# Second router in lots of two chunks, and transfers moved ahead at the seams of two expert stages

## The chip, the cores and the metric

One core of a Trainium2 chip. The metric is the device time of one execution in microseconds (us), as the median of several runs. The kernel is one launch: a stack of layers on 64 sequences of 64 positions with 256 features (4096 tokens), all in fp32.

## The reference

Cut to what matters here, with `x` of shape (64, 64, 256):

```python
x = x + attention(conditioned_scan(x, cond))
x = x + ffn0(modulated_linear(x, cond))
x = x + mamba(rnn(x))
x = x + swiglu_experts(shared_and_routed_experts(x, cond))
```

The last line is the subject. Its inner part is a mixture of experts (`_L1_cond2_ref`): a router takes the two best of eight experts for each token from sigmoid scores of the token and of `cond`; the routed experts compute `gelu(x W1) W2` with 256 hidden features; two shared experts, which all tokens pass, compute `(silu(x s1) * (x s3)) s2` with 512 hidden features each; the sum of both parts is divided by 4. Its outer part (`_L1_ffn_ref`) takes that result as its tokens: scores `xt @ Wg.T`, again the two best of eight, experts `(silu(x W1) * (x W2)) W3` with 704 hidden features, their outputs weighted with the scores themselves. The final line adds the residual.

## The kernel before

**Stages.** The program runs the layers one after the other. Tokens are handled in `NCH` = 8 chunks of `CH` = 512; a chunk holds `TT` = 4 groups of 128 tokens (one token to a partition), and `NTT` = 32 groups are all tokens. The residual lies in DRAM (`g.x`, which the profile calls x_mid), features on partitions.

**Mamba with the shared experts beside it.** `mamba` walks over the eight chunks, 32 steps (`STEPS`) each. A step is an exponential on ACT (L871), a product on POOL (`hb`, L864), two scans on DVE (L903), a product on DVE (L905), and transposes that gather the result on PE (L919), with one broadcast matmul `cb` (L818) for the step after. `finish` and `project` (L826 to L844) end a chunk: they make the layer's output, add it to the residual, and store that to x_mid. In a chunk's loop the pieces of a generator, `Mixture.beside` of the chunk before, are taken at the end of each step: `BESIDE` = 56 pieces spread over the 32 steps (L941). What is left of the generator runs at the end of the chunk (L943), behind `urgent`, which holds `project`. These pieces are: scores of the first router (L1389), after half of the chunks the choice of experts (`choose`, L1401), the sending of rows of an earlier chunk to the experts' regions (`send`, L1429, whose rows are scattered at L1100), and the matmuls of the shared experts (L1459 for s1 and s3, L1475 for s2), whose rows are stored to a DRAM buffer, shared_rows (L1481).

**The rest of the first router.** After mamba, `Mixture.rest` (L1484) reads the last chunk back (`xlast`), scores it, chooses for the second half of the tokens, sends the chunks 4 to 7, and runs the last chunk's shared experts between.

**Routing.** `Routing.choose` works on n groups of 128 tokens at once: about 27 small DVE operations, two matmuls (L1067, L1068) and a cast on POOL (L1076) give each token and each of its two experts a row in a DRAM buffer with a region for each expert (moe_x for the first, ffn_x for the second). `Routing.send` scatters a chunk with eight indirect DMAs on POOL's queue (L1100). `Routing.tiles` (L1123) turns the counts into a table of at most `NTL` = 39 tiles of 256 rows: expert and first row of each.

**Expert tiles.** `Experts.run` (L1204) goes over the 39 tiles. `load(i)` reads the tile's two table entries into registers of SP's queue, and issues the loads of the expert's weights and of the tile's rows `gx` (L1107) there; the load of rows waits for all scatters of that router. `turn` transposes the rows (L1224), `up` and `down` are the two matrix products, and `give` scatters the results to a DRAM buffer by token (L1112, on POOL). Load(i+2) is issued between `up(i)` and `down(i)`. `Gelu` is the first router's, with weights `r`; `Swiglu` the second's, with weights `w`.

**Combination and second router.** For each chunk, `Mixture.combine` reads the chunk's shared rows (L1503) into a tile x2 and the two routed rows of each token (`fetch`, L1120, 1 MB a chunk, into one of three buffers `rows2`), and adds them on DVE (L1507). `Gate.chunk` (L1520) transposes the sum, scores it (L1182 to L1192), chooses (n = 4 groups), and scatters the chunk. The tiles x2 have three buffers and are what the scatters read. After all chunks come `tiles` and the Swiglu tiles. The final loop (L1559) reads for each chunk the two expert rows of each token (rows3, three buffers) and the residual (x3, three buffers), transposes and sums on PE (L1569), adds on DVE (L1578) and stores.

**What sets the order.** A scheduler that goes by program order as priority and by due times puts the instructions of each engine into one fixed order[...]. Direct loads and stores all go through SP's queue, in order, and a load that waits holds what is behind it. Pools give tiles their memory: a pool opened in memory that another pool has just given up waits for that pool's last readers.

Of the kernel before, what the change touches and what calls it, by code (L numbers as in the profile page):

```python
# [19 lines left out]
P = 128  # L20
# [663 lines left out]
def mamba(g, w, hs, beside):  # L684
# [11 lines left out]
    LEFT = 40  # L696
    BESIDE = 56
    nc.scalar.activation(w.A, w.A, AF.Exp)
    nc.vector.tensor_scalar(w.A, w.A, -1.0, None, ALU.mult)
    hs2 = hs.rearrange("p k b t -> p k (b t)")  # L700
    seq = lambda t: t.rearrange("p (b l) -> p b l", l=L)
    with (
# [186 lines left out]
        for s in range(LAST):  # L889
# [45 lines left out]
            while left < (j + 1) * LEFT // (STEPS - AHEAD):  # L935
# [4 lines left out]
                mid = got  # L940
            for _ in range((j + 1) * BESIDE // STEPS - j * BESIDE // STEPS):  # L941
                next(others, None)
# [6 lines left out]
NE = 8  # L949
# [59 lines left out]
class Routing:  # L1009

    def __init__(self, g, pool, x, name, most):

        nc = g.nc
        self.g, self.x, self.name, self.most = g, x, name, most
        self.sent, self.made = [], []
# [20 lines left out]

        self.goes_on = pool.tile([P, NE, most], F32, name="goes_on")
        nc.gpsimd.memset(self.goes_on, 1.0)  # L1040
        nc.gpsimd.memset(self.goes_on[:, :, 0:1], 0.0)

        self.row = pool.tile([P, 2, NTT], mybir.dt.int32, name="row")

    def choose(self, t0, sel, tags, work):


        nc = self.g.nc
        n = self.most
        wide = lambda t: t.unsqueeze(1).to_broadcast([P, n, NE])  # L1050
# [9 lines left out]
        nc.vector.tensor_tensor(mine, by(masks[0]), by(masks[1]), ALU.add)  # L1060
        nc.vector.tensor_tensor_scan(flat(upto), flat(self.goes_on), flat(mine), 0.0, ALU.mult, ALU.add)
        nc.vector.tensor_sub(mine, upto, mine)
# [133 lines left out]
class Experts:  # L1196
# [6 lines left out]

    def run(self, tables):  # L1204
        g, nc = self.g, self.g.nc
        S = TR // P
        table, rank = tables

        def load(i):
            v = SimpleNamespace()  # L1210
            SP = mybir.EngineType.SP
            e = in_order(g.tc, table[0:1, 0, i : i + 1], [SP], NE - 1)
            row = in_order(g.tc, table[0:1, 1, i : i + 1], [SP], NE * REG)
            self.weights(v, e)
            v.x = self.pw.tile([P, S, RW], F32, name="gx")
            self.routing.read(v.x, row)
            v.i, v.rank = i, rank[:, i : i + 1]
            return v

# [30 lines left out]

        now = load(0)
        turn(now)
        after = load(1)
        for i in range(NTL):
            self.up(now)
            if i + 1 < NTL:
                turn(after)
            nxt = load(i + 2) if i + 2 < NTL else None
            down(now)
            now, after = after, nxt  # L1260
# [94 lines left out]
class Mixture:  # L1355

    HALF = NCH // 2

    def __init__(self, g, pool, x):
        nc, a = g.nc, g.a
        self.g = g
        self.routing = Routing(g, pool, x, "moe", NTT // 2)
        self.Wr = pool.tile([P, 2 * KD, NE], F32, name="Wr")
# [18 lines left out]
    def beside(self, c, x, work):  # L1384

        g = self.g
        pt = scores(g, work, self.Wr[:, :KD, :], x, self.cond[:, ts(c, CB)])  # L1389
        g.nc.scalar.copy(self.score[:, ts(c, TT), :], pt)  # L1390
        yield
        if (c + 1) % self.HALF == 0:
            self.choose(c // self.HALF, work)
            yield
        if c >= self.HALF:
            yield from self.send(c - self.HALF, work)
            if c == NCH - 2:
                yield from self.send(c - self.HALF + 1, work)
        yield from self.shared(c, x, work)

    def choose(self, half, work):  # L1401
        nc = self.g.nc
        n = NTT // 2
        t0 = half * n
        s = work.tile([P, n, NE], F32, name="score")
# [78 lines left out]
    def rest(self, work):  # L1484

        g = self.g
        x = work.tile([P, KD, CH], F32, name="xlast")
        g.nc.sync.dma_start(x, g.x[:, :, (NCH - 1) * CH :])
        pt = scores(g, work, self.Wr[:, :KD, :], x, self.cond[:, (NCH - 1) * CB :])
        g.nc.scalar.copy(self.score[:, (NCH - 1) * TT :, :], pt)  # L1490
        self.choose(1, work)
        others = self.shared(NCH - 1, x, work)
        for c in range(self.HALF, NCH):
            for _ in self.send(c, work):
                for _ in range(4):
                    next(others, None)
        for _ in others:
            pass

    def combine(self, c, rows, work):  # L1500

        nc = self.g.nc
        nc.sync.dma_start(rows, self.made[ts(c, CH), :].rearrange("(t p) d -> p t d", p=P))  # L1503
        got = work.tile([P, TT, 2, D], F32, name="rows2")
        self.routing.fetch(c, got)
        for j in range(2):
            nc.vector.tensor_add(rows, rows, got[:, :, j, :])  # L1507


class Gate:  # L1510


    def __init__(self, g, pool, x):
# [3 lines left out]
        nc.sync.dma_start(self.Wg, g.a["ffn1_WgT"].rearrange("(k p) n -> p k n", p=P))  # L1517
        self.routing = Routing(g, pool, x, "ffn1", TT)

    def chunk(self, c, rows, work):  # L1520
# [7 lines left out]
        pt = scores(g, work, self.Wg, x)  # L1528
        s = work.tile([P, TT, NE], F32, name="score")
        sel = work.tile([P, TT, NE], F32, name="gsel")  # L1530
        nc.vector.tensor_copy(s, pt)
        nc.vector.tensor_copy(sel, s)
        masks = self.routing.choose(c * TT, sel, rows[:, :, D:], work)
        for j in range(2):
            mine = work.tile([P, TT, NE], F32, name="mine")
            nc.vector.tensor_mul(mine, s, masks[j])
            nc.vector.tensor_reduce(rows[:, :, WT + j], mine, AX.X, ALU.add)
        self.routing.send(c, rows)


def mixtures(g, mix, x, out):

    nc, tc = g.nc, g.tc
    with ExitStack() as ctx:
        pool = lambda name, bufs: ctx.enter_context(tc.tile_pool(name=name, bufs=bufs))
        p1 = pool("e1", 1)
        gate = Gate(g, p1, x)
        with ExitStack() as first:
            pool1 = lambda name, bufs: first.enter_context(tc.tile_pool(name=name, bufs=bufs))
            q1, q2, q3, qw = pool1("q1", 1), pool1("q2", 2), pool1("q3", 3), pool1("qw", 3)  # L1550
            mix.rest(q2)
            Gelu(g, mix.routing, (q2, q3, qw)).run(mix.routing.tiles(q1))
            for c in range(NCH):
                rows = q3.tile([P, TT, RW], F32, name="x2")
                mix.combine(c, rows[:, :, :D], q3)
                gate.chunk(c, rows, q2)
        p2, p3, pw = pool("g2", 2), pool("g3", 3), pool("gw", 3)
        Swiglu(g, gate.routing, (p2, p3, pw)).run(gate.routing.tiles(p1))
        for c in range(NCH):  # L1559
            rows = p3.tile([P, TT, 2, D], F32, name="rows3")  # L1560
            gate.routing.fetch(c, rows)
            x = p3.tile([P, KD, CH], F32, name="x3")
            nc.sync.dma_start(x, g.x[:, :, ts(c, CH)])
            for k in range(KD):
# [25 lines left out]
def tile_adaln_attn_ffn_d2(ctx: ExitStack, tc: tile.TileContext, a: dict, out: bass.AP):  # L1590
# [18 lines left out]
    ffn0(g, w_ffn0)  # L1609

    p_hs, close_hs = scoped(tc, "hs", side="right")
    hs = p_hs.tile([P, KD, B, L], F32, name="hs")
    rnn(g, w_rnn, hs)
    close_mid()
    close_x()
    p_mix, close_mix = scoped(tc, "w_mix")
    mix = Mixture(g, p_mix, rows[0])
    close_banks()
    with tc.tile_pool(name="beside", bufs=1) as work:
        mamba(g, w_mamba, hs, lambda c, x: mix.beside(c, x, work))  # L1620
    close_hs()
    close_banks = banks(g)

    mixtures(g, mix, rows[1], out)
    close_banks()
    close_mix()
    close_mamba()

# [77 lines left out]
```

## Time and profile before

| | us |
|---|---|
| median of 3 runs | 3241.16 (3240.91 to 3246.52) |
| the profiled execution | 3242.95, of it 3241.2 in the profiled span |
| mamba, last scan (L903) | ends 2117.6 |
| first scatter and last scatter of `rest` | 2173.5, 2225.2 |
| Gelu tiles: first matmul, last scatter | 2242.8, 2424.9 |
| second router: first scatter, end of last scatter | 2447.2, 2545.6 |
| Swiglu tiles: first transpose, last scatter | 2557.3, 3183.2 |
| end of the span | 3241.2 |

Times in the lower rows are counted from the start of the span. They come from the timeline and the rows of single lines. In a group's row, "x64 | 64.3, 1005 | 20.5 <-issue 17.1" says: 64 instructions, 64.3 us busy, 1005 ns each, 20.5 us in which the engine stood idle just before them, most of it not put down to another engine. In a row of waits, "28.0, 6, 9.0" are the total, the number and the longest. The engines are PE (matmul), PEld (its weight load), DVE, ACT, POOL and SP (which issues DMAs).

### The profile page before, as it was taken

Reading aid. Unit: us, or ns where it says so; the run is one execution under the profiler, and the core shown is the slowest. Engines: PE = TensorE matmul, PEld = TensorE weight load, DVE = VectorE, ACT = ScalarE, POOL = GpSimd, SP = SyncE. Lnnn points to the kernel's source line nnn. Section 1 sums busy time; section 2 is a strip of 40 time slices with the busy share of each in tenths; the row PEclk is TensorE's granted clock in tenths of the full one; section 3 lists DMA queues with packets and bytes.
Section 4 is the critical chain, followed back from the end, with each engine's and each line's share of the span. In section 5 each row is a group of like instructions: output and inputs, shape, how many; then the busy total and the mean of one; then the engine's idle time right before and its main releaser. Section 6 shows DMA issues by size and latency. Waiting matters only on the chain. (4 is left out here: it accounts for less than half of the span.)

```text
span 3241.2 us, 38871 instructions
## 1 busy us (share of the span) xinstructions
PE 2586.4 (80%) x13918; PEld 1807.0 (56%) x13932; DVE 1757.8 (54%) x2860; ACT 1421.5 (44%) x2380; POOL 1308.3 (40%) x1091
## 2 busy tenths in 40 slices
PE   1978886777957788888778888677984599999995
PEld 1534443445734455555455555555761388888885
DVE  0166556884049988898978797731335322222221
ACT  0444443775456575766566666522331112222220
POOL 0011213542046766767577777824445311111110
PEclk9889997878967899999889899898996799999997
DMA  9598000000111212121122122224765655555545
GB/s 220 185 374 331 2 2 0 17 20 30 40 40 64 80 63 75 56 81 69 56 69 82 62 89 73 85 71 134 234 201 186 205 172 168 170 175 169 167 137 195
DMA packets 246305, 376.59 MB, mean 116 GB/s; under 512 B 45712, under 2 KB 147152, under 8 KB 245856
## 3 DMA queue, kind: packets, MB, share of 16 engines
q1 hardware_dynamic: 232480, 336.60, 32.1%
q0 software_dynamic: 13632, 37.50, 3.1%
q8 instruction: 110, 1.80, 0.2%
q14 instruction: 83, 0.68, 0.1%
HBM read 250.81 MB, written 123.22 MB: 115 GB/s over the span
## 5 line engine op out<-in xcount | busy, mean ns | idle before, releaser
L864 POOL TENSOR_TENSOR hb<-dx,Bn 128x1024 f32<-128x1024 f32 x256 | 601.1, 2358 | 267.2 <-PE yp L919 257.1
L903 DVE TENSOR_TENSOR_SCAN hb<-dA,hb 128x512 f32<-128x512 f32 x512 | 603.5, 1210 | 50.1 <-ACT dA L871 47.5
L871 ACT ACTIVATE dA<-delta,A 128x504 f32<-128x504 f32 x512 | 344.1, 683 | 293.4 <-DVE hb L903 290.7
L919 PEld LDWEIGHTS yp<-ident,hb 128*128 128x128 f32 x2048 | 270.1, 153 | 167.5 <-issue 128.1
L1335 PE MATMUL ps<-gxT,w 128*128 128x256 f32 x1560 | 360.3, 387 | 0.8 <-DVE gxT L1226 0.8
L905 DVE TENSOR_TENSOR hb<-hb,cb 128x1024 f32<-128x1024 f32 x256 | 312.3, 1220 | 78.6 <-PE cb L818 60.9
L1335 PEld LDWEIGHTS ps<-gxT,w 128*128 128x128 f32 x1560 | 292.7, 191 | 63.0 <-issue 25.2
L1459 PE MATMUL mq<-x,moe_s 128*128 128x256 f32 x896 | 258.5, 423 | 59.0 <-ACT up L1466 44.3
L919 PE MATMUL yp<-ident,hb 128*128 128x128 f32 x2048 | 304.4, 293 | 1.0 <-ACT yT L931 1.0
L1112 POOL DMA_INDIRECT ffn_y<-gy,to x78 | 74.8, 959 | 563.8 <-ACT gy L1248 559.4
L1339 DVE TENSOR_TENSOR gh<-gs,ps 128x256 f32<-128x256 f32 x195 | 81.2, 417 | 322.0 <-ACT gs L1338 321.1
L1459 PEld LDWEIGHTS mq<-x,moe_s 128*128 128x128 f32 x896 | 176.1, 212 | 121.1 <-ACT up L1466 51.4
L1247 PE MATMUL acc<-w,gh 128*128 128x256 f32 x936 | 230.1, 388 | 0.6 <-ACT gy L1248 0.6
L354 POOL TENSOR_TENSOR E<-E,z 128x1024 f32<-128x1024 f32 x32 | 60.8, 1900 | 417.3 <-DMA moe_x<-fill 204.8
L1248 ACT ACTIVATE gy<-acc,wt 128x256 f32<-128x256 f32 x156 | 73.9, 473 | 341.9 <-PE acc L1247 341.9
L1247 PEld LDWEIGHTS acc<-w,gh 128*128 128x128 f32 x936 | 168.4, 189 | 44.7 <-issue 25.5
L818 PE MATMUL cb<-parts,pick 80*128 80x512 bf16 x256 | 106.7, 417 | 94.7 <-DVE hb L905 79.5
L1338 ACT ACTIVATE gs<-ps 128x256 f32<-128x256 f32 x195 | 74.7, 383 | 231.7 <-PE ps L1335 226.3
L1236 DVE TENSOR_TENSOR to<-at,pick 128x2 int32<-128x2 f32 x78 | 12.6, 161 | 219.5 <-DMA ffn_y<-gy,to 125.5
L1112 POOL DMA_INDIRECT moe_y<-gy,to x78 | 74.8, 959 | 123.4 <-ACT gy L1248 121.0
L372 PE MATMUL acc<-oT,Wout 128*128 128x512 f32 x256 | 114.9, 608 | 9.3 <-ACT oT L366 9.3
L1475 PE MATMUL mq<-moe_s,sh 128*128 128x256 f32 x448 | 116.3, 398 | 4.8 <-ACT up L1466 4.8
(387 smaller groups left out, 4661.6 us busy)
## 6 DMA issues: line engine op xcount, KB each, us to landing
w<-in_ffn_W_dram SPq DMA_DIRECT2D x117, 640.0 KB, 4.6
Bn<-B SPq DMA_DIRECT2D x128, 512.0 KB, 3.6
moe_x<-fill SPq DMA_DIRECT2D x129, 260.0 KB, 5.0
ffn_x<-fill SPq DMA_DIRECT2D x129, 260.0 KB, 6.2
r<-in_moe_r_dram SPq DMA_DIRECT2D x78, 256.0 KB, 3.3
gx<-moe_x SPq DMA_DIRECT2D x39, 260.0 KB, 3.5
gx<-ffn_x SPq DMA_DIRECT2D x39, 260.0 KB, 4.1
x<-x_mid SPq DMA_DIRECT2D x16, 512.0 KB, 5.0
```

Source lines behind the costliest of these rows:

```text
L372: nc.tensor.matmul(ps, wa.Wout[:, o, ts(k, P)], v.o[:, o], start=(o == 0), stop=(o == H // 2 - 1))
L818: nc.tensor.matmul(t, pick[:, n : n + 1].to_broadcast([rows, P]), v.parts, start=True, stop=True)
L864: nc.gpsimd.tensor_mul(hb, vs[c].dx[p], Bn[:, n % NB, :].unsqueeze(1).to_broadcast([P, PI, CH]))
L871: nc.scalar.activation(decays[s][i][:, :, 1:], seq(vs[c].delta[p][:, i, :])[:, :, 1:], AF.Exp, scale=w.A[:, p * PI + i, n : n + 1],)
L903: ins = nc.vector.tensor_tensor_scan(h, dA[i].rearrange("p b l -> p (b l)"), h, 0.0, ALU.mult, ALU.add)
L905: ins = nc.vector.tensor_tensor(hb, hb, cb.unsqueeze(1).to_broadcast([P, PI, CH]), ALU.mult)
L919: nc.tensor.matmul(yp[i][:, t, :], hb[:, i, ts(t, P)], g.ident, start=(n == 0 and t == 0), stop=(n == S - 1 and t == CH // P - 1), is_tran ...
L1112: i = self.g.nc.gpsimd.indirect_dma_start(out=self.y, out_offset=bass.IndirectOffsetOnAxis(ap=to, axis=0), in_=y, in_offset=None)
L1247: nc.tensor.matmul(po[:, s, :], h, w, start=(i == 0), stop=(i == len(parts) - 1))
L1335: nc.tensor.matmul(ps[:, j, :], v.w12[:, k, ts(j * full + i, P)], v.xT[:, k, :], start=(k == 0), stop=(k == KD - 1))
L1459: nc.tensor.matmul(ps[:, i % 2, :], w[:, k, ts(i, P)], xu[:, k, :], start=(k == 0), stop=(k == KD - 1))
L1475: nc.tensor.matmul(ps[:, t, :], h[:, i, ts(t, P)], self.s2[:, i, :], start=(i == 0), stop=(i == NS - 1))
```

## The change

Six edits, all in the two mixtures and what stands next to them.

- In mamba's last chunk 72 pieces are taken beside the steps where the other chunks take 56.
- The first router keeps its lots and sends; they are written as tables (`LOTS`, `SENDS`).
- The second router chooses for two chunks at once (`LOT` = 2, n = 8 groups): `chunk` only scores, and every second chunk `lot` chooses, writes the tags into both chunks' rows with ACT, and sends both. Two copies and a cast of scores go from DVE to ACT.
- The shared rows of all chunks have a tile each (`x2_0` to `x2_7`), read by one function, which `Experts.run` of the Gelu tiles calls after it has issued the loads of tiles 0 and 1 (its new argument `then`). The residual chunks likewise have a tile each (`x3_0` to `x3_7`), read after the loads of Swiglu tiles 0 and 1.
- `load` is split: the weights of tiles 0 and 1 are issued first, and then the rows of tile 0 and of tile 1 (`load_rows`). The pool of the Swiglu weights, `gw`, is opened before the Gelu tiles, so that it takes over no memory of theirs; the tables of the second router are made inside the first part's scope.
- The mixture's weights (`w_mix`) are given memory on the side from which `hs` is taken, before the recurrent layer, and mamba's weights are given up before `mixtures`.

```diff
@@ mamba
+    BESIDE_LAST = 72
...
-            for _ in range((j + 1) * BESIDE // STEPS - j * BESIDE // STEPS):
+            most = BESIDE if c + 1 < NCH else BESIDE_LAST
+            for _ in range((j + 1) * most // STEPS - j * most // STEPS):
                 next(others, None)
@@ Routing
-        n = self.most
+        n = sel.shape[1]
@@ Experts
-    def run(self, tables):
+    def run(self, tables, then=lambda: None):
...
         def load(i):
-            v = SimpleNamespace()
-            SP = mybir.EngineType.SP
-            e = in_order(g.tc, table[0:1, 0, i : i + 1], [SP], NE - 1)
-            row = in_order(g.tc, table[0:1, 1, i : i + 1], [SP], NE * REG)
-            self.weights(v, e)
+            v = SimpleNamespace(i=i, rank=rank[:, i : i + 1])
+            self.weights(v, in_order(g.tc, table[0:1, 0, i : i + 1], [SP], NE - 1))
+            return v
+
+        def load_rows(v):
+            row = in_order(g.tc, table[0:1, 1, v.i : v.i + 1], [SP], NE * REG)
             v.x = self.pw.tile([P, S, RW], F32, name="gx")
             self.routing.read(v.x, row)
...
-        now = load(0)
+        now, after = load(0), load(1)
+        load_rows(now)
         turn(now)
-        after = load(1)
+        load_rows(after)
+        then()
@@ Mixture
+    def shared_rows(self, c, rows):
+        self.g.nc.sync.dma_start(rows, self.made[ts(c, CH), :].rearrange("(t p) d -> p t d", p=P))
+
     def combine(self, c, rows, work):
...
-        nc.sync.dma_start(rows, self.made[ts(c, CH), :].rearrange("(t p) d -> p t d", p=P))
@@ Gate.chunk
-        s = work.tile([P, TT, NE], F32, name="score")
-        sel = work.tile([P, TT, NE], F32, name="gsel")
-        nc.vector.tensor_copy(s, pt)
-        nc.vector.tensor_copy(sel, s)
-        masks = self.routing.choose(c * TT, sel, rows[:, :, D:], work)
+        nc.scalar.copy(self.score[:, ts(c, TT), :], pt)
+        self.rows[c] = rows
+        if (c + 1) % self.LOT == 0:
+            self.lot(c // self.LOT, work)
+
+    def lot(self, i, work):
+        nc = self.g.nc
+        n = self.LOT * TT
+        s = self.score[:, ts(i, n), :]
+        sel = work.tile([P, n, NE], F32, name="gsel")
+        nc.scalar.copy(sel, s)
+        tags = work.tile([P, n, RW - D], F32, name="gtags")
+        masks = self.routing.choose(i * n, sel, tags, work)
         for j in range(2):
-            mine = work.tile([P, TT, NE], F32, name="mine")
+            mine = work.tile([P, n, NE], F32, name="mine")
             nc.vector.tensor_mul(mine, s, masks[j])
-            nc.vector.tensor_reduce(rows[:, :, WT + j], mine, AX.X, ALU.add)
-        self.routing.send(c, rows)
+            nc.vector.tensor_reduce(tags[:, :, WT - D + j], mine, AX.X, ALU.add)
+        for c in range(i * self.LOT, (i + 1) * self.LOT):
+            rows = self.rows.pop(c)
+            nc.scalar.copy(rows[:, :, D:], tags[:, ts(c % self.LOT, TT), :])
+            self.routing.send(c, rows)
@@ mixtures
         gate = Gate(g, p1, x)
+        pw = pool("gw", 3)
...
-            q1, q2, q3, qw = pool1("q1", 1), pool1("q2", 2), pool1("q3", 3), pool1("qw", 3)
-            mix.rest(q2)
-            Gelu(g, mix.routing, (q2, q3, qw)).run(mix.routing.tiles(q1))
+            q1, qw = pool1("q1", 1), pool1("qw", 3)
+            with tc.tile_pool(name="rest", bufs=2) as work:
+                mix.rest(work)
+            q2, q3, qr = pool1("q2", 2), pool1("q3", 3), pool1("qr", 1)
+            rows = [qr.tile([P, TT, RW], F32, name=f"x2_{c}") for c in range(NCH)]
+
+            def shared_rows():
+                for c in range(NCH):
+                    mix.shared_rows(c, rows[c][:, :, :D])
+
+            Gelu(g, mix.routing, (q2, q3, qw)).run(mix.routing.tiles(q1), shared_rows)
             for c in range(NCH):
-                rows = q3.tile([P, TT, RW], F32, name="x2")
-                mix.combine(c, rows[:, :, :D], q3)
-                gate.chunk(c, rows, q2)
-        p2, p3, pw = pool("g2", 2), pool("g3", 3), pool("gw", 3)
-        Swiglu(g, gate.routing, (p2, p3, pw)).run(gate.routing.tiles(p1))
+                mix.combine(c, rows[c][:, :, :D], q3)
+                gate.chunk(c, rows[c], q2)
+            tables = gate.routing.tiles(p1)
+        p2, p3 = pool("g2", 2), pool("g3", 3)
+        px = pool("gx", 1)
+        xs = []
+
+        def residual_chunks():
+            for c in range(NCH):
+                x = px.tile([P, KD, CH], F32, name=f"x3_{c}")
+                nc.sync.dma_start(x, g.x[:, :, ts(c, CH)])
+                xs.append(x)
+
+        Swiglu(g, gate.routing, (p2, p3, pw)).run(tables, residual_chunks)
         for c in range(NCH):
...
-            x = p3.tile([P, KD, CH], F32, name="x3")
-            nc.sync.dma_start(x, g.x[:, :, ts(c, CH)])
+            x = xs[c]
```

## The prediction

> **What bounds the kernel now.** I read the busy times by stage first, since the share over the whole span mixes limits. Columns: window, then PE, PEld, DVE, ACT and POOL busy, the granted PE clock, the DMA share, GB/s.
>
> ```profile
> 2133.00:2166.00 33.00, 15.90 (x60) 10.03 (x59) 5.07 (x17) 4.13 (x7) 5.42 (x28) 0.84 0.36 120
> 2166.00:2243.00 77.00, 54.17 (x232) 44.36 (x232) 11.91 (x47) 20.91 (x30) 42.81 (x48) 0.85 0.29 97
> 2243.00:2424.00 181.00, 165.13 (x776) 133.01 (x776) 62.70 (x305) 60.22 (x117) 74.57 (x79) 0.99 0.72 218
> ...
> 2447.00:2546.00 99.00, 36.83 (x119) 14.66 (x119) 49.60 (x227) 11.63 (x20) 66.31 (x76) 0.62 0.45 150
> 2546.00:2557.20 11.20, 0.00 (x0) 0.00 (x0) 0.12 (x1) 0.00 (x0) 0.00 (x0) 0.50 0.84 263
> 2557.20:3184.00 626.80, 623.80 (x2808) 509.28 (x2808) 151.60 (x546) 127.54 (x313) 74.60 (x78) 0.99 0.50 164
> 3184.00:3241.20 57.20, 26.20 (x128) 24.10 (x128) 10.65 (x16) 0.00 (x0) 0.20 (x1) 0.58 0.79 268
> ```
>
> The tiles (2243 to 2424 and 2557 to 3184) are bound by PE. The change works on the seams between them. At 2546 to 2557 nothing computes; after 3184 the DMA is busiest.
>
> In the second router (2424 to 2560) the groups of instructions put POOL first:
>
> ```profile
> L1100 POOL DMA_INDIRECT ffn_x<-x,row x64 | 64.3, 1005 | 20.5 <-issue 17.1 <-POOL row L1076 3.4
> L1076 POOL CAST row<-rowf 128x8 int32<-128x8 f32 x8 | 1.5, 189 | 20.7 <-DVE rowf L1075 20.6
> L1052 POOL COPY x<-number 128x4 f32<-128x4 f32 x5 | 0.9, 190 | 12.1 <-DMA ffn_x<-x,row 12.1
> ```
>
> 64 scatters at a pace of 1.266 us (0.96 and 0.30 to the next, from the timeline) are 81.0 us. The first starts at 2447.21 and the last ends at 2545.63: 98.4 us, so 17.4 us are gaps, mostly row buffers that come free late (12.1 us on L1052).
>
> The waits before the Swiglu tiles, then those of the final combination:
>
> ```profile
> PE ps L1224 <- DMA gx<-ffn_x: 23.3, 1, 23.3
> ```
>
> ```profile
> PE acc L1569 <- DMA rows<-ffn_y: 28.0, 6, 9.0
> DVE x L1578 <- DMA x<-x_mid: 25.9, 4, 8.3
> ```
>
> Both stand at transfers. And the end of mamba, groups of instructions from the last scan (2117.6) to 2156:
>
> ```profile
> L1459 PE MATMUL mq<-x,moe_s 128*128 128x256 f32 x40 | 10.0, 385 | 1.5 <-ACT up L1466 1.5
> ...
> L1475 PE MATMUL mq<-moe_s,sh 128*128 128x256 f32 x32 | 7.2, 383 | 0.7 <-ACT up L1466 0.7
> ...
> L1182 PE MATMUL ps<-xlast,Wr 128*8 128x512 f32 x2 | 1.9, 1036 | 7.6 <-DMA xlast<-x_mid 7.6
> ```
>
> 72 matmuls of shared experts stand between the last scan and the last chunk's router.
>
> [...] the last scatter ends at 2545.63 and the first weight load that waits for it is issued at 2547.56, 1.93 us later. [...] the trace has 0.19 us for the 128x32 rows. [...]
>
> **Part 1, the last mamba chunk (L941).** 72 pieces go beside the 32 steps instead of 56. In the compiled order 40 matmuls of shared experts are left after the last scan's cb instead of 72: 32 x 0.385 = 12.3 us of PE time move under the scans. Two thirds of these lay on the path: project's last add is at 2132.93, leftover runs to 2147, SP must pass the store of the leftover rows (2147.83) and Wg's load (2150.08) before xlast at 2150.51, and PE has it at 2154.75. After it, the leftover is interleaved with project, which ends near 2137 (8 pairs x 2 x 0.385 is 6 us, part of it in PE's waits); the store and its receipt give xlast's issue at 2140.5, and with the 4.2 us it takes now PE goes on at 2144.7: -10. Cost: 16 more pieces in the chunk. Cover: it has 110.6 us of PE in 148.6 us, the chunk before it 123.7 in 148.0 without being longer; 110.6 + 12.3 stays below that. Without cover all 12.3 come back. The scatters of sends (2) and (3) now come as 8 and 8 in POOL's order where they came 4, then two hb products, then 12: 8 x 1.266 = 10 us in which POOL makes no hb; DVE waited about 11 us at this place before. 0 to +6; I take +1. Sum -9, bounds -13 and 0.
>
> **Part 2, the start of the Gelu tiles.** On SP the reads of shared rows x_0 and x_1 stand ahead of the first table entries, and wait for the first router's scatters, whose memory they take over: so first weights are not ahead of those scatters. The total for the table (2228.63) lies behind PE's shared matmuls as before. The reads go out at about 2228, under the table's DVE work to 2235. Second weights stand before gx0 (two r of 0.26 MB: 1.6 us at 341 GB/s), and six shared reads (3.1 MB, 9.2 us) before tile 2's inputs, with tile 2 due after 2 x 4.47 us: about 1 us of stall. The 341 GB/s are a mean over fully loaded slices just after 2546. Sum +2.5, bounds 0 and +8.
>
> **Part 3, the second router.** Removed: eight reads of shared rows from this stage (4.2 MB) and their wait for row buffers; four of eight chains of about 27 small DVE operations (each lot's are 64 wide, 0.22 against 0.19 us: 4 x 27 x 0.22 = 24 us instead of 8 x 27 x 0.19 = 41, at one place hidden under scatters anyway). The 17.4 us of gaps should shrink to three lot changes of about 0.6 us. But the first scatter waits for two chunks, and in DVE's compiled order the adds of chunks 4 to 7 lie inside lot 0's chain: chunk 7's first add stands before rowf. With three rows2 buffers its fetch goes out only after chunk 4's adds. Now: c0's fetch is in by 2433.2, c3's goes out at 2435.7 and, at 8 us, lands near 2443.7; c4's near 2447, c7's goes out near 2449.5 and lands near 2457.5. Its add (1.2), the rest of the chain and the cast: first scatter at 2462, 15 us later than now. Then 81.0 + 1.8 from 2462.4: end at 2545.2 against 2545.63: -0.4. Bounds -6 (fetches at 6 us) and +6.
>
> **Part 4, the start of the Swiglu tiles.** The tables already ended at 2540.3, before the last scatter; only the loads gain. w(0) and w(1) (2.16 MB each) go out before the last scatters, having buffers of their own. After the last one: 1.9 receipt, 2.6 for a gx alone, PE at +4.6 instead of 2557.30 - 2545.63 = 11.67: -7.0; bounds -8 and -5. Queued behind gx0 and gx1 on SP: eight residual reads (4.2 MB) and then w(2): 4.2 + 2.2 + 0.3 = 6.7 MB, 19.6 us at 341 GB/s. Tile 2 is due 2 x 15.9 us after the start: hidden, by 12 us; uncovered it would cost up to 8, if scatters halve the rate.
>
> **Part 5, the final combination.** Five of eight x reads fell into this stage: 2.6 of its 15.35 MB. The rest at its own 268 GB/s takes 47.5 us (-9.7); at 341 GB/s with 2.6 to start and 2 for the last store, 41.6 (-15.6). What is late next is rows<-ffn_y, held by three buffers and behind the out stores on SP. Walking the SP order gives a last add 11 us earlier: I take -11.3, bounds -15 and -7.
>
> The first weights of the mixture and the moved rcond matmuls: nothing; they landed before B<-dbc (922) in any case. If not covered, at most one load's landing, 5 us.
>
> **Sum.** -9 + 2.5 - 0.4 - 7.0 - 11.3 = -25.2 us, against the profiled execution's 3242.95 us (span 3241.2 and 1.75 around it): 3217.75. The median of the runs is 1.79 lower, so 3216.0. Bounds added in quadrature give about 10 us either way: 3206 to 3226 for this case.
>
> **Rivals.**
> A. The adds of later chunks don't hold lot 0, and only the gaps go. For it: POOL has 17.4 us of gaps. Against it: the order on DVE is fixed. First scatter at about 2447, end near 2530: 15 us more, 3201.
> B. The gain is eaten at three places: hb waits for POOL's scatters (+5), the tile 2 stall at Gelu (+3.5), rows<-ffn_y takes over the waits of x<-x_mid (+4). For it: PE waits 28.0 us for rows<-ffn_y already. Against it: the sum of bytes falls. 3216 + 12.5 = 3228.5.
> C. Slower: lot 0 behind chunk 7's fetch, at the head of the second router. POOL then has no gaps to give, so each us by which the first scatter is later is a us of the whole. It decides from 2494 on (2462 + 32 for 3248). That needs 16 us for each of the two fetches in series instead of 8, or a third fetch in series. For it: the fetches wait for one another's buffers. Against it: 8.0 us was measured with shared reads beside them. About 3250.
> D. It doesn't do what it says: w(0) and w(1) stay behind the scatters of the second router, as the first router's do. Then -7 is lost and the other terms stay: 3223, inside the range.
>
> **How the numbers follow.** The main case, D within it, 0.60; A 0.12; B 0.16, of which 0.04 ends within 0.2%; sundry cancelling to no change 0.05; C 0.07. A measurement of this kernel tells about 0.2% (6.5 us) from no change. Faster 0.84, same 0.09, slower 0.07. The range goes from A's middle (3200) to past B (3236).
>
> **What would show it.** PE's first matmul on xlast 9 us earlier counted from the last scan; first scatter L1100 15 us later counted from the last Gelu scatter and then no wait on L1052; 4 to 5 us from the last L1100 to PE L1224 with w landed before; no DVE wait for x<-x_mid and a stage after the last ffn_y scatter of 46 us. I am wrong if lot 0's chain runs before chunk 7's add, if a step of the last chunk grows, or if tile 2 of either expert stage stalls.

## The result, and the profile after

| | us |
|---|---|
| before, median of 6 runs of the first comparison | 3242.45 (3240.91 to 3247.97) |
| changed, median of 6 runs | 3221.53 (3211.95 to 3226.11) |
| ratio | 0.993, 95% interval 0.9914 to 0.9946 |
| profiled execution of the changed kernel | 3220.07, span 3218.3 |

The change is 20.9 us faster where 25.2 were forecast. How large the gain is depends on more than the code, as the control below shows: in a later group of runs the same kernel was only 8.7 us faster than the kernel before, measured on the same chip as it.

The busy times by stage of the changed kernel, with the columns of before (window, length, PE, PEld, DVE, ACT, POOL, granted PE clock, DMA share, GB/s). The windows begin and end at the instructions that bound the stages, so they are not the windows of before:

```profile
2119.30:2145.20 25.90, 18.94 (x81) 12.69 (x80) 5.29 (x7) 2.78 (x5) 6.36 (x26) 0.96 0.19 65
...
2234.70:2421.40 186.70, 168.27 (x780) 134.78 (x780) 64.46 (x312) 61.60 (x118) 73.97 (x77) 0.97 0.74 227
2421.40:2456.90 35.50, 14.12 (x58) 6.92 (x58) 23.04 (x42) 6.42 (x16) 2.28 (x3) 0.71 0.69 243
2456.90:2538.90 82.00, 19.66 (x82) 8.50 (x79) 21.02 (x99) 10.86 (x29) 62.77 (x69) 0.67 0.44 155
2538.90:2543.40 4.50, 0.00 (x0) 0.02 (x1) 0.00 (x1) 0.00 (x0) 0.00 (x0) 0.50 0.37 107
2543.40:3169.40 626.00, 622.67 (x2808) 507.58 (x2808) 151.62 (x546) 127.84 (x313) 74.80 (x78) 1.00 0.51 168
3169.40:3218.30 48.90, 22.43 (x128) 20.66 (x128) 11.00 (x16) 0.00 (x0) 0.00 (x0) 0.72 0.76 260
```

The stretch in which nothing computes ahead of the Swiglu tiles has shrunk to 4.5 us. In the second router a long start (35.5 us from the last Gelu scatter to the first scatter) is followed by scatters without a gap; the groups of POOL in it:

```profile
L1104 POOL DMA_INDIRECT ffn_x<-x,row x64 | 61.9, 967 | 19.4 <-issue 15.8 <-DMA ffn_x<-x,row 2.1 <-POOL row L1080 1.1
L1080 POOL CAST row<-rowf 128x16 int32<-128x16 f32 x4 | 1.7, 430 | 32.9 <-DVE rowf L1079 32.9
L1056 POOL COPY gtags<-number 128x8 f32<-128x8 f32 x2 | 0.4, 212 | 0.0
```

The wait for row buffers (12.1 us on the copy of `number`) is gone. In its place POOL waits once, 32.9 us, for the first lot. The waits of the final stage:

```profile
DVE x L1625 <- PE acc L1616: 42.1, 16, 16.4
PE acc L1616 <- DMA rows<-ffn_y: 24.3, 5, 8.9
```

DVE waits for the residual no more; PE waits for rows<-ffn_y nearly as long as before (28.0 then).

The same stages in numbers, each from the start of an instruction to the start of another. The last column is the control, a later run of the same program. In the kernel before, 2117.6 us is where the last scan starts; the table of the kernel before gives it as its end, which is 2118.8.

| from, to | before | changed | difference | control |
|---|---|---|---|---|
| start, first scan of mamba | 945.8 | 950.5 | +4.7 | 950.4 |
| first scan, last scan | 1171.8 | 1168.8 | -3.0 | 1168.8 |
| last scan, PE on xlast | 37.1 | 25.9 | -11.2 | 26.1 |
| PE on xlast, last moe_x scatter | 70.5 | 70.8 | +0.3 | 70.7 |
| last moe_x scatter, PE on gx | 15.7 | 18.7 | +3.0 | 18.0 |
| PE on gx, last moe_y scatter | 184.0 | 186.7 | +2.7 | 188.6 |
| last moe_y scatter, first ffn_x scatter | 22.3 | 35.5 | +13.2 | 36.2 |
| first, last ffn_x scatter | 97.5 | 81.0 | -16.5 | 92.5 |
| last ffn_x scatter, PE on gx | 12.6 | 5.5 | -7.1 | 13.7 |
| PE on gx, last ffn_y scatter | 625.9 | 625.0 | -0.9 | 626.0 |
| last ffn_y scatter, end | 58.0 | 49.9 | -8.1 | 51.0 |
| span | 3241.2 | 3218.3 | -22.9 | 3242.0 |

Stages that a given edit does not touch differ too between runs: up to the first scan the profiles of the changed kernel's variants gave 942.5 to 951.3 us, and the 1168.8 us of mamba's loop were 1167.4 to 1179.3 in them with the same code. So the +4.7 and -3.0 can't be put down to the change, and below the seams are compared, not only the whole.

### The profile page after: what moved, and what is told of

Its sections match the earlier page's. It is cut to its first block, busy times and chain, and to the rows that moved or that the text cites. A ratio compares the mean times of both kernels' runs of the same rounds, so it can differ in the third digit from the quotient of the medians.

```text
span 3218.3 us, 38646 instructions
## 1 busy us (share of the span) xinstructions
PE 2582.8 (80%) x13910; PEld 1808.0 (56%) x13924; DVE 1740.6 (54%) x2740; ACT 1426.8 (44%) x2401; POOL 1305.8 (41%) x1083
```

## The experiments

They ran in three groups, each with the kernel before on the same chip: medians of it were 3247.6, 3248.44 and 3246.51 us. "Against before" means against these.

**56 pieces in the last chunk** (first group).

```diff
-    BESIDE_LAST = 72
+    BESIDE_LAST = 56
```

> The changed kernel with 56 pieces beside the last chunk's steps again (part 1 undone). Theory: the 72 pieces bought time only at the tail; from the last scan to PE on xlast it takes 37 us again instead of 25.9, the loop itself is no shorter by more than 2 us, and the whole is 9 to 11 us longer than the changed kernel. Rival (the pieces were paid for inside the loop): the loop from first to last scan gets shorter by 6 us or more, and the whole changes by less than 4 us.

Measured: 3235.23 us, 12.4 below before (ratio 0.996, 0.9947 to 0.9973). The loop took 1169.1 us, within its spread, so no shortening shows either. From the last scan to PE on xlast it took 30.3 us: neither 37 nor 25.9. On the same chip the experiment "Residual read in the final loop" below, which undid nothing, lies 12.0 us below before, so the whole is not the 9 to 11 us longer that were expected either. Both theories fall. The groups of instructions from the last scan on, in this kernel:

```profile
L1472 PE MATMUL mq<-x,moe_s 128*128 128x256 f32 x40 | 10.0, 384 | 1.5 <-ACT up L1479 1.5
...
L1488 PE MATMUL mq<-moe_s,sh 128*128 128x256 f32 x32 | 7.2, 382 | 0.7 <-ACT up L1479 0.7
...
L1186 PE MATMUL ps<-xlast,Wr 128*8 128x512 f32 x4 | 1.9, 593 | 0.7 <-ACT up L1492 0.7
```

The 72 left-over matmuls are all there, as before, and yet PE waits for no DMA at xlast. Up to this point the code differs from the kernel before only in where tiles and pools get their memory (`w_mix`, `rest`, mamba's weights, `gw`) and in the width of the second router's constants. POOL's waits there, of before and then of this kernel, tell what that changed:

```profile
POOL onesb L1022 <- DMA shared_rows<-up: 9.0, 1, 9.0
```

```profile
POOL onesb L1024 <- PE mp L842: 5.7, 1, 5.7
```

Before, the first write into the second router's constants waited for the landing of the left-over pieces' last store (issued at 2147.83), from which it takes no data. The reading is that it was to go where that store still read, and with other memory the wait is gone. Wg, in the same pool, waited with it on SP, and xlast behind Wg, until 2150.51. In this experiment the write waits for `project` alone, Wg goes out at 2135.50, and xlast at 2141.80, under the left-over matmuls. Up to the matmul of the counts (total, which ends `rest`) it took 111.0 us from the last scan before, 101.4 in this experiment and 100.1 in the changed kernel. So the new memory, with 56 pieces, is enough for 9.6 of the 10.9 us, and the 16 pieces add 1.3. Only about 2.3 us of that is the landing itself (2147.83 to 2150.08). The rest is that Wg and xlast, free of the store, now stand ahead of it in SP's order. SP's queue, before and then in the changed kernel:

```profile
2147.83 0.36 SPq L1481 DMA_DIRECT2D shared_rows<-up  x1
2150.08 0.37 SPq L1517 DMA_DIRECT2D Wg<-in_ffn_WgT_dram  x1
2150.51 0.46 SPq L1488 DMA_DIRECT2D xlast<-x_mid  x1
```

```profile
2138.03 0.38 SPq L1532 DMA_DIRECT2D Wg<-in_ffn_WgT_dram  x1
2138.71 0.36 SPq L847 DMA_DIRECT2D x_mid<-x  x1
2139.11 0.47 SPq L1494 DMA_DIRECT2D shared_rows<-up  x1
2141.54 0.36 SPq L1501 DMA_DIRECT2D xlast<-x_mid  x1
```

Part of what the pieces save PE gives back at once: it then stands idle 6.8 us for xlast's landing, and its four router matmuls take 1046 ns each in place of 593.

The other corner, 72 pieces with the old memory, was not run, so the split holds only in this order. An estimate from the changed kernel's trace: its left-over store is issued at 2139.11. With the 2.25 us of landing and the 0.43 us from Wg to xlast that the trace of before shows, xlast would go at 2141.8. It goes at 2141.54, when the store to x_mid has landed. By this estimate the pieces alone would have bought nearly as much.

**Lots of one chunk** (first group).

```diff
-    LOT = 2
+    LOT = 1
```

> The changed kernel with lots of one chunk in the second router; all else as changed. Theory: the lots cost at the head and gain nothing later, because POOL's scatters are the bound. With one chunk a lot the compiled DVE order puts chunk 5's first add ahead of the end of lot 0's chain, not chunk 7's: first scatter about 7 us earlier after the last Gelu scatter (28 instead of 35.5), four more lot changes of 0.6 us, the whole 4 to 6 us shorter than the changed kernel. Rival (fewer DVE instructions are what closed POOL's gaps): gaps of over 8 us come back between the scatters and the whole is 2 us or more longer.

Measured: 3237.91 us, 9.7 below before (0.9972, 0.9962 to 0.9982). The first scatter came after 29.6 us instead of 35.5: as expected from DVE's order. But the scatters took 93.3 us, and in this run as in the others of the group ACT showed waits in this stage that the changed kernel's first profile has not (see the control). The next experiment undid nothing, as it turned out, and so stands for the changed kernel on this chip: this kernel is 2.3 us longer than it, within the spread, where 4 to 6 us shorter were expected. The experiment settles the head of the stage, not the rest.

**Residual read in the final loop** (first group).

```diff
-        Swiglu(g, gate.routing, (p2, p3, pw)).run(tables, residual_chunks)
+        Swiglu(g, gate.routing, (p2, p3, pw)).run(tables)
...
-            x = xs[c]
+            x = px.tile([P, KD, CH], F32, name=f"x3_{c}")
+            nc.sync.dma_start(x, g.x[:, :, ts(c, CH)])
```

> The changed kernel with the residual of each chunk read in the final loop again, into buffers of its own (part 5 undone, without the three-buffer limit of before). Theory: the 4.2 MB come back into a stage bound by transfers; final stage (last ffn_y scatter to end) 54 to 58 us instead of 49.9, nothing gained at the Swiglu start, the whole 4 to 8 us longer. Rival (three rows3 buffers and the stores bound the stage, and not the bytes): the final stage stays within 2 us of the changed kernel's.

Measured: 3235.63 us, 12.0 below before (0.9972, 0.9961 to 0.9984); final stage 50.0 us. This looks like the rival, and is a miss of mine: nothing held the eight reads, so the compiled order put them beside the Swiglu tiles by itself, from 2566 to 2598 us. The experiment undid nothing. A second one with three buffers does.

**Swiglu weights late** (first group).

```diff
-        pw = pool("gw", 3)
...
-        p2, p3 = pool("g2", 2), pool("g3", 3)
+        p2, p3, pw = pool("g2", 2), pool("g3", 3), pool("gw", 3)
```

> The changed kernel with the pool of the Swiglu weights opened after the first mixture's pools are closed, as it was: first weights wait for the last scatters again (part 4 undone, residual reads still ahead). Theory: from the end of the last L1104 scatter to PE's first transposes 11 to 12 us instead of 4.5, the whole 6 to 8 us longer. Rival (the reads of rows and residuals bound the start, not the weights): less than 3 us.

Measured: 3242.61 us, 5.0 below before (0.9986, 0.9975 to 0.9996). That is 7.0 us longer than the experiment just above, which stands for the changed kernel on this chip (the spread of the two leaves about 1 to 12 us), and as expected. From the last scatter to PE on gx it took 20.7 us, and 10.4 to 16.2 in the other three kernels of this group, whose weights start early. The direction agrees, but the stage varies too much to give a size. That all four stand far above the 5.5 us of the changed kernel's first profile was not expected, and led to the control.

**The changed kernel again, as the control** (second group).

> The changed kernel itself, unedited, as the control of this group. In the four runs before this one ACT stood in 15 to 23 us of waits in the second router whose releaser the profile calls remote, and the scatters had gaps of 6 to 12 us; the profiles of the kernel before and of the changed kernel had none. If the edits caused it, this run has none: scatters 81 us from first to last, the whole 20 us below the kernel before. If it belongs to the chip or the execution, it has them too: 86 to 90 us from first to last scatter, 10 to 16 us below the kernel before.

Measured: 3239.75 us, 8.7 below before (0.9976, 0.9961 to 0.9991). The program that took 81.0 and 5.5 us in two stages took 92.5 and 13.7. It is not the edits. ACT's waits in the second router, from the last Gelu scatters on:

```profile
ACT up L1190 <- remote: 12.7, 2, 8.5
ACT up L1190 <- PE ps L1186: 12.2, 6, 2.9
ACT gscore L1548 <- remote: 10.8, 2, 5.7
ACT x2T L1546 <- remote: 5.0, 1, 5.0
```

"remote" is the profile's word for a releaser that it doesn't find among the core's own. 28.5 us of such waits hold the third lot's scores, and POOL runs dry. SP is next. Its timeline at the first weights, in the first profile of the changed kernel and then in the control:

```profile
2500.16 0.39 SPq L1330 DMA_DIRECT2D w<-in_ffn_W_dram  x1
2500.75 0.38 SPq L1331 DMA_DIRECT2D w<-in_ffn_W_dram  x1
2501.31 0.37 SPq L1330 DMA_DIRECT2D w<-in_ffn_W_dram  x1
```

```profile
2535.40 0.71 SPq L1330 DMA_DIRECT2D w<-in_ffn_W_dram  x1
2538.22 0.00 SPq L1331 DMA_DIRECT2D w<-in_ffn_W_dram  x1
2541.04 0.01 SPq L1330 DMA_DIRECT2D w<-in_ffn_W_dram  x1
2543.89 0.73 SPq L1331 DMA_DIRECT2D w<-in_ffn_W_dram  x1
2548.12 0.70 SPq L1334 DMA_DIRECT2D w<-in_ffn_W_dram  x1
```

The issues stand 0.6 us apart in one and 2.8 to 4.3 in the other. In between are register instructions, which the page doesn't count. In the trace they take 0.03 to 0.05 us each in the first; in the second 11 of 18 take 0.64 to 0.72. The issues also begin later, 15.9 us before the start of the last scatter and not 37.7, because the tile table waits for the late lots. The weights are then not all ahead of the last scatters, and gx0, behind them on SP, is late.

**Shared rows in the second router** (second group).

```diff
-            Gelu(g, mix.routing, (q2, q3, qw)).run(mix.routing.tiles(q1), shared_rows)
+            Gelu(g, mix.routing, (q2, q3, qw)).run(mix.routing.tiles(q1))
             for c in range(NCH):
-                mix.combine(c, rows[c][:, :, :D], q3)
-                gate.chunk(c, rows[c], q2)
+                rows = q3.tile([P, TT, RW], F32, name="x2")
+                mix.shared_rows(c, rows[:, :, :D])
+                mix.combine(c, rows[:, :, :D], q3)
+                gate.chunk(c, rows, q2)
```

> The changed kernel with the shared rows read in the second router again, into three buffers, and lots of two chunks kept (the read ahead undone). Theory: Gelu regains 5 us (tiles start 3 us earlier after the last scatter, tile 2 without a stall), the second router loses the row buffers: lot 1 waits for chunk 0's scatters, gaps of 15 us or more between the scatters; the whole 8 to 15 us longer than the control. Rival (the read ahead only pays what it costs): within 3 us of the control.

Measured: 3257.69 us, 9.2 above before (1.0038, 1.002 to 1.0055) and 17.9 above the control. Scatters from first to last 121.4 us instead of 92.5; the Gelu tiles 185.8 instead of 188.6. POOL and then SP say why:

```profile
L1080 POOL CAST row<-rowf 128x16 int32<-128x16 f32 x4 | 0.8, 196 | 65.3 <-DVE rowf L1079 55.1 <-DVE n_e L1140 10.2
```

```profile
SPq L1514 <- DMA ffn_x<-x,row: 48.9, 6, 22.5
```

Reads of shared rows wait on SP for scatters to give up their buffers, and fetches wait behind them. The first tile did not start earlier, as was expected: 17.8 us after the last scatter, the control 18.0. Lots of two chunks with three row buffers are slower than the kernel before. A buffer for each chunk is what makes the lots possible.

**Residual in three buffers** (second group).

```diff
-            x = xs[c]
+            x = p3.tile([P, KD, CH], F32, name="x3")
+            nc.sync.dma_start(x, g.x[:, :, ts(c, CH)])
```

> The changed kernel with the residual in three buffers, as before: three chunks are read ahead, five in the final loop behind the stores (part 5 undone; in e3_residual_late the compiled order had put the reads ahead by itself, so it did not undo it). Theory: final stage from the last ffn_y scatter to the end 57 to 58 us instead of 50, the whole 7 to 8 us longer than the control. Rival (rows3 and the stores bound the stage): final stage under 52 us.

Measured: 3247.11 us (0.9996, 0.9984 to 1.0007), 7.4 above the control; final stage 56.9 us against the control's 51.0, with DVE's wait for x<-x_mid back:

```profile
DVE x L1617 <- DMA x<-x_mid: 25.2, 4, 8.1
```

By the stage part 5 is worth 5.9 us here, and 8.1 by the first profile.

**Lots of one chunk, adds held back** (second group): a dependency without a semaphore keeps DVE's adds of chunk c behind the choice of chunk c-2.

```diff
-    LOT = 2
+    LOT = 1
...
-            nc.vector.tensor_add(rows, rows, got[:, :, j, :])
+            i = nc.vector.tensor_add(rows, rows, got[:, :, j, :])
+            if behind is not None:
+                self.g.tc.add_manual_dep(i.ins, behind, info, reason="not ahead of an earlier lot's choice")
```

> The changed kernel with lots of one chunk, and the adds of chunk c kept behind the choice of chunk c-2 in DVE's order. Theory (the late first scatter is the price of the compiled order and of the lots): first scatter 23 us after the last Gelu scatter instead of 35.5, seven changes of chunk at 0.6 us, stage from last Gelu scatter to last ffn_x scatter 105 to 108 us instead of 116.5, the whole 8 to 11 us below the control. Rival (with one chunk a lot the chain of small operations can't keep up with eight scatters, 10.1 us): gaps of 10 us or more, no gain.

Measured: 3234.45 us, 14.0 below before (0.9956, 0.9937 to 0.9975), 5.3 below the control. The first scatter comes after 24.2 us, where 23 were expected: the theory's cause of the late head holds. The scatters then take 99.2 us; ACT's nameless waits, 23.9 us of them, are in this run too, so the rival isn't refuted by it.

**All final fetches ahead** (third group): eight rows3 tiles, fetched before the loop.

```diff
+        got = []
         for c in range(NCH):
-            rows = p3.tile([P, TT, 2, D], F32, name="rows3")
-            gate.routing.fetch(c, rows)
+            got.append(px.tile([P, TT, 2, D], F32, name=f"rows3_{c}"))
+            gate.routing.fetch(c, got[c])
+        for c in range(NCH):
+            rows = got[c]
             x = xs[c]
```

> The changed kernel with eight rows3 tiles in the final loop, all fetches ahead of the stores on SP. Theory for why the final stage came out at 49.9 us and not at the forecast 46.7: with three rows3 buffers, fetches 4 to 8 stand behind out stores on SP that wait for DVE, and the DMA engines idle in between; all eight fetched at once the stage takes 40 to 44 us. Rival (the bytes at the rate of the stage bound it): 48 us or more.

Measured: 3211.89 us, 34.6 below before (0.9888, 0.9869 to 0.9908). Final stage 39.0 us. The busy times of its window, in the columns of the stages above:

```profile
3172.00:3212.00 40.00, 17.68 (x129) 16.43 (x128) 10.99 (x16) 0.47 (x1) 0.96 (x1) 0.81 0.85 318
```

318 GB/s where the changed kernel has 260: the stage was held by SP's order and three buffers. No ACT stalls in this group: scatters 81.2 us, PE's start 5.9 us after them.

**Shared rows later** (third group): on SP, behind the row loads of tiles 10, 12, ... 24.

```diff
+        i = self.g.nc.sync.dma_start(rows, self.made[ts(c, CH), :].rearrange("(t p) d -> p t d", p=P))
+        self.g.tc.add_manual_dep(i.ins, self.routing.reads[10 + 2 * c], info, reason="beside the tiles, one at a time")
```

> The changed kernel with the eight reads of shared rows on SP behind the row loads of Gelu tiles 10, 12, ... 24 instead of around tiles 0 to 2. Theory: the 5.7 us that the Gelu stage lost are those reads in front of the first loads; tiles start 16 us after the last scatter of the first router instead of 18.7, and last 184 us from first transposes to last scatter instead of 187 to 189; the whole 4 to 6 us shorter. Rival (the second weights ahead of gx0 and the new order of loads cost it): less than 2 us.

Measured: 3224.22 us, 22.3 below before (0.9927, 0.9911 to 0.9944). Tile 2 took 5.3 us from scatter to scatter, as before, where the changed kernel took 9.8: that stall was the reads'. But the tiles beside which the reads now go took 4.6 to 6.0 us instead of 4.5, and the stage as a whole 188.6. In 2300 to 2380 us the DMA moved 271 GB/s instead of 234, and a load of `r` landed in 3.9 us instead of 3.2. From the first moe_y scatter to the last it took 176.4 us, much as in the changed kernel (176.6), and 173.9 before: the reads cost about 2.6 us in either place. (With no reads here, in the experiment with three row buffers, it took 173.8; with the reads at the start, 175.7 to 179.1 in the profiles.) And the start stayed at 18.1 us without any read ahead of it: gx0 is issued 3.2 us after the first `r` instead of 1.75, and PE has it 4.2 us later instead of 3.3, because the second tile's weights now go first. My theory holds for tile 2 alone.

**All three** (third group): one-chunk lots with ordered adds, shared rows later, fetches ahead.

> All three together: lots of one chunk with ordered adds, shared rows later, all final fetches ahead. If the parts add: 5 (lots, as measured on the control's chip) + 5 + 7 = 17 us below the changed kernel on the same chip, some 22 to 26 us below the kernel before there. If the stages hand delays on: less than 12 below the changed kernel.

Measured: 3205.01 us, 41.5 below before (0.987, 0.9853 to 0.9886), and the fastest kernel here. The changed kernel was not in this group; against the kernel with the final fetches alone it is 6.9 us faster, by medians of four runs each. In the second router the first scatter comes 11.7 us earlier than with shared rows later alone (24.5 for 36.2), but 4.3 us come back between the scatters (85.5 for 81.2) and 3.5 at the Swiglu start (9.2 for 5.7): the first weights now load over the last scatters, and gx0 is issued 5.2 us after the last one ends, not 1.9. The stage hands most of the gain on to the next: of 11.7 us 3.9 are left.

**Pauses between the scatters** (third group).

```diff
+            p = self.g.nc.gpsimd.iota(self.rest, [[1, 1024]], base=c, channel_multiplier=0, allow_small_or_imprecise_dtypes=True)
+            self.g.tc.add_manual_dep(p.ins, i.ins.name, info, reason="behind the scatters")
```

> The changed kernel with one iota of about 2 us on POOL behind every eight scatters of the second router. The runs without row-buffer gaps showed ACT and SP stalls in that stage in most profiles, and the two with gaps (the kernel before, and e5_shared_three) none. If back-to-back scatters starve the two engines: no remote waits of ACT, scatters at 81 + 14 = 95 to 97 us from first to last, PE's Swiglu start within 7 us after the last. If gaps have nothing to do with it: stalls as in the control, 100 us or more, start 12 us or more after the last scatter.

Measured: 3226.39 us, 20.1 below before (0.9946, 0.9926 to 0.9966). No nameless wait of ACT, scatters 87.4 us, PE's start 5.7 us. But in this group the two kernels without pauses and without lots changed have none either, so it decides nothing about their cause. The pauses cost 6.2 us and not 14: each iota took 1.0 us, half of what was meant.

## Why the prediction was right, and where it wasn't

The sum came out within 5.5 us of the measured median, in part by luck. By the stages of the one profile the five parts give -24.0 us for -25.2, but four of them were off by 2.2 to 3.2 us, two each way. And the stalls that the control shows were not in this profile; with them, in the control's group, 8.7 us of gain are left.

**Part 1, right in size, the cause only in part.** Forecast -10 at the tail, found -11.2. What was wrong is the price of nothing for the moved weights. The store of the left-over rows did hold xlast, as the prediction says, but it held it through memory that the next pool took over, and the edit frees that memory: with 56 pieces and the new memory 9.6 of the 10.9 us up to the counts are already there. That the pieces alone would have done it too is the estimate above, not shown. I read POOL's wait for shared_rows<-up in the waits of before and did not ask what POOL's constants had to do with that store. The +1 for the loop was not seen (1168.8 and 1169.1 us with 72 and 56 pieces), but with a spread of 1167.4 to 1179.3 it could not be.

**Part 2, too small.** +2.5 forecast, +5.7 found. That first weights stay behind the scatters was right. gx0 is issued 2.9 us after the first `r` instead of 1.75, so 1.2 us later for the 1.6 forecast; its landing under more loads (about 1.7 us more) was left out. Tile 2's stall was put at about 1 us; its scatters come 4.5 us later than before, of which the tiles around give back 1.9. Spreading the reads shows that they cost the Gelu tiles 2.6 us in either place: with the DMA busy 72% of the time there was cover for their bytes, but not for loads that arrive later.

**Part 3, right at both ends.** First scatter 13.2 us later (forecast 15), scatters then back to back, 82.0 us from the first's start to the last's end for 81.0 and 1.8 of changes: -3.3 against -0.4, within the bounds of 6. The 0.22 us for a small operation 64 wide was not shown by the trace of before, which has 0.19 at 128x32; that of the changed kernel has 0.22 at 128x64 (L969 to L975), and 5.9 us for the whole chain of lot 1 (2460.86 to 2466.73). In DVE's order seven of the eight adds of chunks 4 to 7 lie between lot 0's first operation (2443.18) and its row numbers (2455.12), chunk 7's first add at 2453.72. Both experiments with one-chunk lots move the head as DVE's order says. So the lots gain nothing by themselves; the row buffers do.

**Part 4, right.** -7.0 forecast, -7.1 found in the first comparison. In its trace the last scatter ends at 2538.82, gx0 is issued 1.92 us later (1.9 forecast, 1.93 to the first weights before), and PE has it 2.67 us after that, where 2.6 were estimated. Late weights cost 7.0 us of the whole against the kernel on the same chip that undid nothing; the stage itself took 5.5 to 18.1 us in the profiles with early weights, so the stalls weigh more there than the edit. Tile 2 of Swiglu did not stall: 607 us from the first to the last ffn_y scatter in every run.

**Part 5, too large.** -11.3 forecast, -8.1 found; 5.9 between three buffers and the control. (The other estimate of this part, 41.6 us at 341 GB/s, sums to 42.0; it was not taken.) The failed step is "walking the SP order gives a last add 11 us earlier". Between fetches the stage did not hold its rate: 260 GB/s, not more than before, so 12.7 of 15.35 MB gave 49 us. That three buffers and the stores on SP do this is shown by the fetches ahead.

**The rivals.** By number D (3223) lies nearest to the 3221.53 us, but it fell in the first profile: the first weights were issued at 2500.16, 37.7 us before the last scatter. Of B, the gain eaten at three places, two came: the stall at Gelu tile 2 and the waits for rows<-ffn_y. Longer hb waits are not seen. A fell with the order on DVE, C's point (2494) was far away from the first scatter (2456.9). The control is near D in effect: the weights' issues were late, slow and not all ahead of the last scatters, though for a cause that no rival had.

**What stays open.** Why ACT, and mostly SP with it, took instructions so slowly in seven of the eight profiles of the first two groups, and in none of the third group and of the first comparison. The exception, shared rows in three buffers, has long gaps between its scatters; whether that is why, the pauses could not tell. What the change is worth in a given group of runs, between 8.7 and 20.9 us here, goes with it: the two stages with the stalls take 20 us more in the control's profile. The kernel before was not profiled in those groups. Open too is how part 1 divides, as 72 pieces with the old memory were not run.

## What to carry to other kernels

A load that stands behind a store may be held by the store's memory as well as by the queue (here POOL waited 9.0 us for a store's landing, and xlast on SP until 2150.51): look who else waits for the same landing, and whether the waiting tile shares a pool's place with the stored one. Where two edits remove the same wait, undo each by itself, or their shares stay unknown. A read moved beside other work is free only while the loads it delays have slack (here eight reads cost the Gelu tiles 2.6 us), so read the landing times of that stage, not only its DMA share. When a seam is closed, walk on to the next: earlier scatters were partly paid back at the weights (3.5 of 11.7 us), and rows<-ffn_y took over from the residual until it was fetched ahead too.

## What the runs showed of the hardware

In the control, between 2535 and 2557 us, 11 of 18 register instructions of SP took 0.64 to 0.72 us instead of 0.03 to 0.05, while POOL issued its scatters every 1.27 us, up to 2552. ACT stood for 4 to 8.5 us before each of six single small copies from 2473 to 2504. The two stages took 20 us more than in the first profile of the same program.

In the control's trace a packet of the instruction queue 14 came at 2506.9 us, 48 us after the first scatter; in the first profile one came at 2476.7, 20 us after it, and ACT had no such wait. In the other four profiles with stalls and lots of two the first packet of this stage came 40 to 45 us after the first scatter, and 21 to 22 in the other three with lots of two and eight row buffers and without stalls. But in the two kernels with lots of one chunk and stalls it came 16 and 19 us after, and ACT stood all the same. So the late packet may as well follow from the stall as cause it; neither is shown.
